# Padding the last 64 tokens to a whole chunk on TensorE, and a plan that lets tiled matmuls follow each other

## The chip, the cores and the metric

The kernel runs on one core of a Trainium2 chip. The metric is the device time of one execution in microseconds. Four engines compute: TensorE (PE in the profile, with its weight loads shown apart as PEld), VectorE (DVE), ScalarE (ACT) and GpSimd (POOL). SyncE (SP) only issues DMA transfers here. Each engine works through its own queue in order and waits on semaphores for the others.

## The reference

The input is 16 images of 56 x 56 pixels with 128 channels in float32. Two layers follow each other.

- Layer 0: a group norm over each image, then attention in shifted windows of 7 x 7 (4 heads of 32 channels, with a position bias and a mask), an output projection, and the residual.
- Layer 1: the 3136 pixels of an image become tokens. A layer norm and a causal linear attention are added (features elu + 1, with running sums over the tokens), then a second layer norm, a 128 x 128 matmul, a batch norm over all tokens of all images, and a recurrence y(t) = sigmoid(w(t) + V y(t-1)) along the tokens; its result is added too.

```python
x = x + _L0_conv_ref(_gn(x), ...)            # windows: q k^T, softmax, times v, w_out
t = _to_tokens(x)
t = t + _L1_attn_ref(_ln_t(t), W, b)         # num/den with cumulative sums of k v^T and k
t = t + _L1_ffn_ref(_ln_t(t), W, V, gamma, beta)   # batch norm, then the recurrence
```

## The kernel before

Everything up to the recurrence is recorded first as steps of a planner (class Plan) and only then emitted. A step names its engine, a cost (how long it holds the engine) and a lag (when its result is ready), a rank, the steps it comes after, and the buffers that it takes and drops. The planner plays the steps through with these costs: every engine takes the ready step of lowest rank whose buffers are free. It does so forwards and backwards up to 30 times, keeps the order that ends first by its own figures, and emits all steps in the order of their starts. So a changed cost gives all five engines a new order of instructions. At run time these orders are fixed; if a step's input is late, its engine stands.

Each image gives the planner three kinds of work:

- turned (line 562 and around it): the image is loaded by groups of tokens into xt_buf, PE transposes each group, ACT copies it into xw_buf, DVE takes statistics; from these come the weights ws and the biases of the window attention (L657 to L706).
- window_row, eight times: DVE gathers a row of 8 windows (gather_windows, L747). PE projects q and k (L757) and v (L784) and makes the scores (L808): 32 matmuls of 32 rows by 49 columns, each on its own tile of the array. DVE adds the mask and finds the maxima, POOL subtracts them, ACT takes exponentials, DVE sums, POOL scales. PE transposes (L863), ACT copies, and PE mixes the values (mix, L882): 32 matmuls of 49 rows by 32 columns. ACT copies the result into oT_buf (L917).
- token_group, seven times: PE projects the windows' output (project, L1054), DVE adds it to the tokens (L1063), then a layer norm (statistics on DVE L958, small steps and the scaling on POOL, L965 to L978, a transpose on PE, L562), feature maps (L1095, ACT L1105 and L1114, DVE L1118), values (L1142), transposed features (L1165), products within a chunk (L1180), the attention from the state and within the chunk (L1209, L1212), the running state (L1220), and after a second layer norm the matmul L1309, whose results are stored for the recurrence.

An image has 3136 tokens: six groups of 4 chunks of 128 tokens, and a last group of one chunk of 64. In that last group the transposes read 64 rows, and the matmuls whose stationary operand is the chunk's tokens have 64 columns. PSUM has 3 single banks (tag b) and 2 double ones (tag a, for scores, transposes, mixes and the token attention), and the planner gives them out.

A float32 matmul appears as two PE instructions, a transpose as one. PE holds 15,735 matmuls and transposes in the program, 27,070 in the profile.

When the plan has ended, the recurrence runs (lines 1464 to 1690): PE, ACT, DVE and the DMA queues in a chain of 112 steps with 16 to warm up.

Of the kernel before, what the change touches and what calls it, by code (L numbers as in the profile page):

```python
# [39 lines left out]
class Step:  # L40


    def __init__(self, engine, cost, rank, emit, after, takes, drops, lag):
        self.engine, self.cost, self.rank, self.emit = engine, cost, rank, emit
        self.takes, self.drops, self.lag = takes, drops, lag
        self.then = []
        self.missing = 0
        for a in after:
            if a is not None:
                a.then.append(self)  # L50
                self.missing += 1


class Plan:
# [8 lines left out]
    AHEAD = 30.0  # L63

# [16 lines left out]
    def run(self, missing, then, rank, gate, begin=None, done=None):  # L81


        events, ready, busy = [], {}, {}
# [14 lines left out]
        while events:  # L99
# [14 lines left out]
            for e, steps in ready.items():  # L114
                if busy[e]:
                    continue
                held, best = [], None
                while steps and best is None:
# [12 lines left out]
                push(t + best.cost, "idle", best)  # L131
                push(t + best.lag + self.HOP, "done", best)
# [74 lines left out]
def tile_conv_attn_hybrid(  # L207
# [32 lines left out]
    assert 0 < T % GT <= CK  # L240
# [36 lines left out]
    def chunks_of(g, xt):  # L277

        return xt[: GROUPS[g][1][0], G * g : G * g + len(GROUPS[g][1]), :]

# [90 lines left out]
    with ExitStack() as s1:  # L371
# [66 lines left out]

        nc.gpsimd.memset(xw_bufs[1], 0.0)
# [118 lines left out]
        def transpose_group(pt, xg):  # L558

            n = xg.shape[0]  # L560
            for cc in range(xg.shape[1]):
                nc.tensor.transpose(  # L562
                    pt[:, n * cc : n * (cc + 1)], xg[:, cc, :], ident[:n, :n]
                )
# [11 lines left out]
        def turned(b, t, loaded, xw_buf, rank):  # L576
# [7 lines left out]
            for g in range(NG):  # L584
# [3 lines left out]
                def turn(g=g, bt=bt):  # L588
                    t0, t1 = group_tokens(g)
                    o[g] = bank(bt, P, t1 - t0)  # L590
                    transpose_group(o[g], chunks_of(g, t["xt"]))
# [17 lines left out]
                def stat(g=g):  # L609
                    if o["st"] is None:  # L610
# [9 lines left out]
                    part(g, (0.43, 0.60), (0.06, 0.23)),  # L620
# [7 lines left out]
                    part(g, (0.62, 0.75), (0.18, 0.30)),  # L628
# [8 lines left out]
                        part(g, (0.62, 0.70), (0.11, 0.19)),  # L637
# [95 lines left out]
        def window_row(b, u, i, o, t, taken, normed, xw_buf, oT_buf, rank):  # L733
# [188 lines left out]
            xk = st("DVE", (0.45, 0.53), rank, gather_windows, [*taken, last_value[i % 2]], drops=[xw_buf])  # L922
# [7 lines left out]
            sc = st("PE", (0.98, 1.06), rank, scores, [q, k, last_turn[i % 2]], takes=[asc], drops=[kT])  # L930
# [10 lines left out]
            mi = st("PE", (0.85, 0.92), rank, mix, [tu, vo], takes=[apa], drops=[pT, v])  # L941
            cost = (0.82, 0.94) if u < NU - 1 else (1.20, 1.32)
# [5 lines left out]
        def layer_scale(t, g, d, key, rank, after, drops=()):  # L948
# [27 lines left out]
            def scale():  # L976
                d["xn"] = own(xn, P, G, C)[:np, :nk]
                nc.gpsimd.tensor_tensor(  # L978
                    d["xn"],
# [5 lines left out]
            def turn():  # L985
                d["pt"] = bank(bt, P, nk * np)
                transpose_group(d["pt"], d["xn"])
# [3 lines left out]
            s = plan.step("POOL", part(g, (2.13, 2.17), (1.20, 1.24)), rank, join, [s])  # L991
            sc = plan.step(
                "POOL",
                part(g, (1.01, 1.05), (0.30, 0.34)),
# [8 lines left out]
                part(g, (0.43, 0.60), (0.06, 0.23)),  # L1003
# [27 lines left out]
        def token_group(b, g, i, t, turned_x, rows_done, oT_buf, xt_buf, rank):  # L1031
# [19 lines left out]
            def project():  # L1051
                d["po"] = bank(bo, np, nk, C)
                for cc in range(nk):
                    nc.tensor.matmul(  # L1054
                        d["po"][:, cc, :],
                        t["oT"][:, t0 + np * cc : t0 + np * (cc + 1)],
# [5 lines left out]
            def plus_attention():  # L1062
# [3 lines left out]
            s0 = st("POOL", part(g, (1.23, 1.27), (0.34, 0.38)), rank - SLOT, plus_bias, [turned_x])  # L1066
            s1 = st(
                "PE",
                part(g, (0.88, 1.04), (0.22, 0.38)),
# [10 lines left out]
            def x_out():  # L1080
                d["xnT"] = own(xnT, P, GT)[:, :nt]
                nc.scalar.copy(d["xnT"], d["pt"])  # L1082
# [6 lines left out]
            def feature(j):  # L1089
# [3 lines left out]
                def proj():  # L1093
# [4 lines left out]
                        d["xnT"],  # L1098
# [17 lines left out]
                def larger():  # L1116
                    d[key] = own(f, P, GT)[:, :nt]
                    nc.vector.scalar_tensor_tensor(  # L1118
                        d[key],
# [7 lines left out]
                p = st("PE", part(g, (0.87, 1.03), (0.12, 0.28)), rank, proj, [xo, *first], takes=[bp], drops=[xnT])  # L1127
                s = st("ACT", part(g, (0.58, 0.68), (0.25, 0.35)), rank, relu, [p], takes=[r])
                s = st("ACT", part(g, (0.53, 0.63), (0.20, 0.30)), rank, expo, [s])
                return st("DVE", part(g, (0.66, 0.75), (0.16, 0.25)), rank, larger, [s], takes=[f], drops=[r, bp]), f  # L1130
# [5 lines left out]
            def chunk(f, cc):  # L1136
                return f[:, np * cc : np * (cc + 1)]

            def values():
                d["pv"] = bank(bv, np, nk, C)  # L1140
                for cc in range(nk):
                    nc.tensor.matmul(  # L1142
                        d["pv"][:, cc, :],
# [15 lines left out]
            s = st("PE", part(g, (0.88, 1.04), (0.22, 0.38)), rank, values, [xo, *first, *last_pd[i % 2]], takes=[bv], drops=[xnT])  # L1159
            vo = st("DVE", part(g, (0.60, 0.69), (0.20, 0.28)), rank, v_out, [s], drops=[bv])  # L1160

            def turn_k():
                d["pk"] = bank(bk, np, nk, C)
# [3 lines left out]
            def k_out():  # L1167
                d["k"] = own(k, P, G, C)[:np, :nk]
# [8 lines left out]
            def products():  # L1177
                d["pA"] = bank(bA, np, nk, np)
                for cc in range(nk):
# [3 lines left out]
                        chunk(d["f0"], cc),  # L1183
# [4 lines left out]
            def A_out():  # L1188
                d["A"] = own(A, P, G, CK)[:np, :nk, :np]
                nc.vector.tensor_tensor(  # L1190
                    d["A"],
                    d["pA"],
                    causal_sb[:np, :np].unsqueeze(1).to_broadcast([np, nk, np]),
# [3 lines left out]
            s = st("PE", part(g, (0.89, 1.05), (0.11, 0.28)), rank, products, [fq, fk], takes=[bA], drops=[bfk])  # L1197
# [5 lines left out]
            def attend(cc):  # L1203
                c = G * g + cc
                if cc == 0:
                    d["pn"] = pairs[apn.place][:np]
                to = d["pn"][:, cc // 2, (C + 1) * (cc % 2) : (C + 1) * (cc % 2 + 1)]
                if c > 0:
# [4 lines left out]
                    to, d["A"][:, cc, :], v1[:np, cc, :], start=c == 0, stop=True  # L1213
                )

            def gather(cc):
                c = G * g + cc
                if c == 0:
# [4 lines left out]
                    v1[:np, cc, :],  # L1223
# [50 lines left out]
            def divisors():  # L1274
                na, ni = max(nk // 2, 1), min(nk, 2)
                pn4 = d["pn"][:, 0:na, 0 : ni * (C + 1)].rearrange(
# [494 lines left out]
```

## Time and profile before

| | |
|---|---|
| median of 3 runs | 1933.95 us (1931.54 to 1940.33) |
| the profiled execution | 1933.64 us, its span 1931.8 us |
| granted clock of TensorE, mean | 0.983 |
| busy, share of the span | PE 96%, PEld 77%, DVE 73%, ACT 68%, POOL 60% |
| planned part | from about 24 us to the first L1521 at 1728.87 us |
| recurrence | from there to the end |

In the profile a line names an instruction's place in the code, its engine, the operation and out<-in by the program's names. The 40 digits of a row are busy tenths in 40 equal slices of the span. The ends of matmuls are modelled, so PE's busy share does not say how much of it is needed; the starts are recorded. In the timeline the columns are start, duration from the first to the last of the merged instructions, engine, line, operation, tile names, rows*columns of the array in use, shape, and count. In the table of groups they are count, then busy us and mean ns of one, then the engine's idle time just before, with what ended it.

### The profile page before, as it was taken

What the parts mean: (1) busy time and instruction counts of PE and PEld (TensorE: products, weight loads), DVE (VectorE), ACT (ScalarE), POOL (GpSimd) and SP (SyncE); (2) the same over time, 40 slices, a digit from 0 to 9 for tenths busy, and PEclk for the clock granted to TensorE, in tenths of its full rate; (3) what the DMA queues carried; (4) which work ended last, traced back from release to release, by engine and by line L of the source; (5) the groups of instructions that cost most, each with busy time, mean ns of one, the idle gap of its engine ahead of it and who ended that gap; (6) DMA issues with size and microseconds to landing.
All of it is one profiled execution on the core that took longest, in us unless ns stands there. A gap on an engine that the chain in (4) does not pass through costs nothing.

```text
span 1931.8 us, 65226 instructions
## 1 busy us (share of the span) xinstructions
PE 1846.2 (96%) x27070; PEld 1489.0 (77%) x27070; DVE 1401.3 (73%) x3227; ACT 1306.1 (68%) x3235; POOL 1159.8 (60%) x2025
## 2 busy tenths in 40 slices
PE   6999999999999999999999999999999999989787
PEld 4878777886887778877878787787878777857666
DVE  5777677777677777776777777767777767757678
ACT  4776766767666777667767676766777766647455
POOL 5766767566667667576767576676757756640000
PEclk8999999999999999999999999999999999989889
DMA  4112121111111121211111111212111020555998
GB/s 134 30 30 70 35 62 36 31 63 41 58 45 48 34 70 30 63 46 59 35 36 58 40 61 33 64 34 65 40 35 42 19 85 19 179 202 191 410 408 291
DMA packets 150462, 160.98 MB, mean 83 GB/s; under 512 B 5456, under 2 KB 134224, under 8 KB 148368
## 3 DMA queue, kind: packets, MB, share of 16 engines
q1 hardware_dynamic: 148576, 155.96, 23.8%
q8 instruction: 215, 3.52, 0.8%
q10 hardware_dynamic: 1584, 0.79, 0.1%
q14 instruction: 87, 0.71, 0.1%
HBM read 80.34 MB, written 76.38 MB: 81 GB/s over the span
## 4 chain that ended last, share of the span: by engine, by line
PE 77%; DVE 8%; ACT 5%; DMA 4%; issue 2%; POOL 2%; SPq 0%; ACTq 0%; DVEq 0%; POOLq 0%
PE bank L757 8%; PE bank L1095 8%; PE bank L784 6%; PE bank L562 6%; PE pair L808 5%; PE pair L863 5%; PE state_bank L1220 5%; PE bank L1054 5%; PE bank L1180 5%; PE pair L1209 4%; PE bank L1142 4%; PE pair L1212 4%; PE pair L882 4%; PE bank L1309 4%; DMA out_dram<-o_a 4%
## 5 line engine op out<-in xcount | busy, mean ns | idle before, releaser
L853 POOL TENSOR_TENSOR p_buf<-p_buf,rc 128x784 f32<-128x784 f32 x128 | 195.1, 1525 | 125.4 <-DVE rc L850 69.5
L834 POOL TENSOR_TENSOR s<-s,mx 128x784 f32<-128x784 f32 x128 | 193.6, 1512 | 102.9 <-DVE mx L831 98.3
L1095 PE MATMUL bank<-xnT,awc_sb 128*128 128x512 f32 (+1 forms) x448 | 210.9, 554 | 2.6 <-ACT xnT L1082 0.9
L1105 ACT ACTIVATE r<-bank,bqk_neg 128x512 f32<-128x512 f32 (+1 forms) x224 | 143.6, 641 | 89.3 <-PE bank L1095 69.8
L1118 DVE SCALAR_TENSOR_TENSOR f<-bank,bqk_one,r 128x512 f32<-128x512 f32 (+1 forms) x224 | 149.9, 669 | 44.3 <-ACT r L1114 36.8
L917 ACT ACTIVATE oT_buf<-pair,gbias 128x28 f32<-128x28 f32 (+4 forms) x576 | 144.1, 354 | 30.6 <-PE pair L882 30.1
L819 DVE TENSOR_TENSOR s<-pair,wmask_sb 128x784 f32<-128x784 f32 x128 | 123.3, 963 | 53.1 <-PE pair L808 41.5
L1209 PEld LDWEIGHTS pair<-state,f 128*128 128x128 f32 (+1 forms) x768 | 121.9, 188 | 48.9 <-issue 29.3
L1220 PE MATMUL state_bank<-v_buf,k 128*128 128x129 f32 x768 | 156.4, 285 | 2.1 <-ACT state L1232 1.7
L1220 PEld LDWEIGHTS state_bank<-v_buf,k 128*128 128x128 f32 x768 | 122.4, 190 | 44.2 <-issue 22.2
L1212 PE MATMUL pair<-v_buf,A 128*128 128x129 f32 (+1 forms) x800 | 155.9, 276 | 0.1
L1209 PE MATMUL pair<-state,f 128*128 128x129 f32 (+1 forms) x768 | 153.5, 281 | 0.3 <-ACT state L1232 0.2
L873 ACT COPY pT<-pair 128x904 f32<-128x904 f32 x128 | 118.5, 926 | 47.5 <-PE pair L863 42.5
L1232 ACT COPY state<-state_bank 128x129 f32<-128x129 f32 x384 | 107.4, 280 | 58.8 <-PE state_bank L1220 54.6
L1044 POOL TENSOR_TENSOR xt_buf<-xt_buf,bout_sb 128x512 f32<-128x512 f32 (+1 forms) x112 | 128.3, 1159 | 30.0 <-PE bank L562 25.9
L1568 ACT ACTIVATE y_a<-z_buf,bsh 128x224 f32<-128x224 f32 x224 | 100.1, 447 | 67.8 <-PE z_buf L1565 66.9
L848 DVE TENSOR_REDUCE sm<-p_buf 128x16 f32<-128x784 f32 x128 | 122.9, 960 | 26.6 <-ACT p_buf L844 25.8
L562 PE MATMUL bank<-ident,xn 128*128 128x128 f32 (+1 forms) x800 | 125.3, 275 | 11.4 <-POOL xn L978 4.0
L1114 ACT ACTIVATE r<-r 128x512 f32<-128x512 f32 (+1 forms) x224 | 130.8, 584 | 3.0
L808 PEld LDWEIGHTS pair<-kT,q_buf 32*49 32x49 f32 x8192 | 105.9, 121 | 30.6 <-issue 18.5
L1565 PE MATMUL z_buf<-y_a,fvT_sb 128*128 128x224 f32 x444 | 127.3, 370 | 0.2 <-ACT y_a L1568 0.2
L831 DVE TENSOR_REDUCE mx<-s 128x16 f32<-128x784 f32 x128 | 122.6, 958 | 1.5
(155 smaller groups left out, 5064.3 us busy)
## 6 DMA issues: line engine op xcount, KB each, us to landing
x_d<-xt_buf SPq DMA_DIRECT2D x96, 256.0 KB, 2.2
xt_buf<-in_x_dram SPq DMA_DIRECT2D x93, 256.0 KB, 2.8
xs_d<-staged SPq DMA_DIRECT2D x15, 1568.0 KB, 6.4
out_dram<-o_a SPq DMA_DIRECT2D x13, 1792.0 KB, 15.3
xw_buf<-x_d SPq DMA_DIRECT2D x8, 2048.0 KB, 22.6
spare<-xs_d SPq DMA_DIRECT2D x4, 1680.0 KB, 17.4
oT_buf<-x_d SPq DMA_DIRECT2D x3, 2048.0 KB, 24.2
xs_ring<-xs_d SPq DMA_DIRECT2D x3, 1680.0 KB, 13.0
```

The lines of the kernel that those rows point to most:

```text
L562: nc.tensor.transpose(pt[:, n * cc : n * (cc + 1)], xg[:, cc, :], ident[:n, :n])
L757: nc.tensor.matmul(d[key], o["ws"][:, j * P : (j + 1) * P], xk, start=True, stop=True)
L808: nc.tensor.matmul(sc[64 * hh : 64 * hh + WT, hp, w * WT : (w + 1) * WT], qT[r : r + HD, w * WT : (w + 1) * WT], d["kT"][r : r + HD, w * W ...
L834: nc.gpsimd.tensor_tensor(d["sf"], d["sf"], d["mx"].unsqueeze(2).to_broadcast([P, nb, WT]), ALU.subtract,)
L853: nc.gpsimd.tensor_tensor(prf, prf, d["rc"].unsqueeze(2).to_broadcast([P, nb, WT]), ALU.mult)
L917: nc.scalar.activation(to, piece, AF.Identity, bias=o["bias"][:, 2:3])
L1095: nc.tensor.matmul(d[f"p{j}"], awc_sb[:, j * P : (j + 1) * P], d["xnT"], start=True, stop=True,)
L1105: nc.scalar.activation(d[f"r{j}"], d[f"p{j}"], AF.Relu, bias=bqk_neg[:, j : j + 1], scale=-1.0,)
L1118: nc.vector.scalar_tensor_tensor(d[key], d[f"p{j}"], bqk_one[:, j : j + 1], d[f"r{j}"], ALU.add, ALU.max,)
L1209: nc.tensor.matmul(to, chunk(d["f0"], cc), t["states"][c], start=True, stop=False)
L1212: nc.tensor.matmul(to, d["A"][:, cc, :], v1[:np, cc, :], start=c == 0, stop=True)
L1220: nc.tensor.matmul(t["pd"], d["k"][:, cc, :], v1[:np, cc, :], start=c == 0, stop=True, skip_group_check=True,)
```

## The change

The last group's single chunk of 64 tokens is handled by PE as a whole chunk. Its transposes read all 128 rows (with zeros or older values behind the tokens), and matmuls whose stationary operand is the chunk take 128 columns; the second half of what comes out is not used. DVE, ACT and POOL still read and write only the 64 tokens. Four memsets at the start make the rows behind the tokens finite. In the planner, scores and mixes are marked as using tiles: after a tiled step PE takes another ready tiled step, if its rank is within 3 of the lowest, and a tiled step behind an untiled one is charged 0.1. Costs and lags of many steps are changed as well.

```diff
+    SWITCH = 0.1
+    NEAR = 3.0
@@ Plan.run
+                if tiles.get(e):
+                    near = sorted(r for r in steps if self.steps[r[1]].tiles)
+                    for r in near:
+                        if r[0] > min(steps)[0] + self.NEAR:
+                            break
+                        s = self.steps[r[1]]
+                        if begin is None or begin(s):
+                            best = s
+                            steps.remove(r)
+                            heapq.heapify(steps)
+                            break
...
-                push(t + best.cost, "idle", best)
-                push(t + best.lag + self.HOP, "done", best)
+                more = self.SWITCH if best.tiles and not tiles.get(e) else 0.0
+                tiles[e] = best.tiles
+                push(t + more + best.cost, "idle", best)
+                push(t + more + best.lag + self.HOP, "done", best)
@@ buffers at the start
+        nc.gpsimd.memset(flat(oT_buf0)[:, T : T + CK], 0.0)
+        for xt in xt_bufs:
+            nc.gpsimd.memset(xt[64:, G * (NG - 1), :], 0.0)
@@ transpose_group
-                    pt[:, n * cc : n * (cc + 1)], xg[:, cc, :], ident[:n, :n]
+                    pt[:, CK * cc : CK * (cc + 1)], xg[:, cc, :], ident
@@ turned
-                    transpose_group(o[g], chunks_of(g, t["xt"]))
+                    xg = whole_chunks(g, t["xt"])
+                    pt = bank(bt, P, CK * xg.shape[1])
+                    o[g] = pt[:, 0 : t1 - t0]
+                    transpose_group(pt, xg)
@@ window_row
-            xk = st("DVE", (0.45, 0.53), rank, gather_windows, ...
+            xk = st("DVE", (0.27, 0.37), rank, gather_windows, ...
-            sc = st("PE", (0.98, 1.06), rank, scores, ...
+            sc = st("PE", (0.88, 0.95), rank, scores, ...
-            mi = st("PE", (0.85, 0.92), rank, mix, ...
-            cost = (0.82, 0.94) if u < NU - 1 else (1.20, 1.32)
+            mi = st("PE", (0.74, 0.81), rank, mix, ...
+            sc.tiles = mi.tiles = True
+            cost = (0.91, 1.04) if u < NU - 1 else (1.47, 1.65)
@@ token_group, project
-                d["po"] = bank(bo, np, nk, C)
+                po = bank(bo, P, nk, C)
+                d["po"] = po[:np]
...
-                        t["oT"][:, t0 + np * cc : t0 + np * (cc + 1)],
+                        t["oT"][:, t0 + CK * cc : t0 + CK * (cc + 1)],
@@ token_group, chunk and products
-                return f[:, np * cc : np * (cc + 1)]
+                return f[:, CK * cc : CK * (cc + 1)]
...
-                        chunk(d["f0"], cc),
+                        chunk(d["f0"], cc)[:, :np],
@@ token_group, attend
-                    d["pn"] = pairs[apn.place][:np]
+                    d["pn"] = pairs[apn.place]
...
-                    to, d["A"][:, cc, :], v1[:np, cc, :], start=c == 0, stop=True
+                    to, d["A"][:, cc, :], v1[:, cc, :], start=c == 0, stop=True
```

The values (L1142) and the tiles k, A and xnT are widened in the same way. Costs of the last group are raised: its transposes from 0.06 to 0.11, its small POOL steps (L965 to L972) from 1.20 to 1.61, and others alike.

## The prediction

> **What bounds the kernel now.** I read the page first, then busy time by stage, then PE's waits, then PE's timeline at the places where the tile shape changes.
>
> ```profile
> span 1931.8 us, 65226 instructions
> ...
> PE 1846.2 (96%) x27070; PEld 1489.0 (77%) x27070; DVE 1401.3 (73%) x3227; ACT 1306.1 (68%) x3235; POOL 1159.8 (60%) x2025
> ...
> PE   6999999999999999999999999999999999989787
> ...
> PEclk8999999999999999999999999999999999989889
> ```
>
> ```profile
> 500.00:900.00 400.00, 394.50 (x6107) 319.36 (x6110) 295.42 (x713) 281.66 (x707) 274.50 (x479) 1.00 0.15 46
> ...
> 1860.00:1932.00 72.00, 58.10 (x364) 50.17 (x364) 57.34 (x96) 39.80 (x89) 0.00 (x0) 0.91 0.87 328
> ```
>
> The second fence gives per stretch the busy time of PE, PEld, DVE, ACT and POOL, the granted clock, the share of the DMA engines and GB/s. From about 24 us to 1729 us the planned part runs: PE is busy in 394.5 of 400 us at clock 1.00, while DVE (295), ACT (282) and POOL (275) have a quarter or more of their time free. From 1729 us on the recurrence runs, some 203 us, with the DMA engines at 0.87 to 1.02; no instruction of it is changed. So the planned part ends when PE has got through its list, and the question is what PE's list costs.
>
> A busy PE hides how. One matmul's record is longer than the time it holds its successor up, so I measure each group of matmuls by its **slot**: from its first start to the first start of the next group. PE's timeline shows them:
>
> ```profile
> 883.92 0.39 PE L1212 MATMUL pair<-v_buf,A 128*128 128x129 f32 x2
> 884.24 0.27 PE L562 MATMUL bank<-ident,xn 64*128 64x64 f32 x1
> 884.44 0.49 PE L1220 MATMUL state_bank<-v_buf,k 128*128 128x129 f32 x2
> 884.86 0.81 PE L882 MATMUL pair<-pT,v 49*32 49x49 f32 x64
> 885.60 0.93 PE L757 MATMUL bank<-oT_buf,ws 128*128 128x392 f32 x2
> 886.36 1.05 PE L1180 MATMUL bank<-f,f 128*128 128x128 f32 x8
> 887.25 1.06 PE L1054 MATMUL bank<-wout_sb,oT_buf 128*128 128x128 f32 x8
> 888.14 0.39 PE L1220 MATMUL state_bank<-v_buf,k 128*128 128x129 f32 x2
> 888.46 0.43 PE L1142 MATMUL bank<-awc_sb,xnT 128*64 128x128 f32 x2
> 888.82 0.49 PE L1209 MATMUL pair<-state,f 128*128 128x129 f32 x2
> 889.15 0.39 PE L1212 MATMUL pair<-v_buf,A 128*128 128x129 f32 x2
> 889.37 0.33 PE L1095 MATMUL bank<-xnT,awc_sb 128*128 128x64 f32 x2
> ```
>
> Read the starts (the numbers behind MATMUL are rows*columns of the array in use). L1212 among full groups (889.15 to 889.37) takes 0.22 us. L1212 ahead of a tiled group (883.92 to 884.24) takes 0.32, L1209 behind one (888.82 to 889.15) 0.33, L1220 between two of them (884.44 to 884.86) 0.42. Over all groups of the planned part the medians are sharp: **entering** a tile shape adds 0.093 us to the full group before it, and **leaving** adds 0.103 us to the full group after it (0.055 where that is a transpose, L562, L863, L1165). The tiled groups hold PE for 0.878 (scores, L808) and 0.738 (mix, L882) whatever stands beside them, the 14 places where these two already touch included. The pieces of the last 64 tokens take 0.202 (L562), 0.363 (L1054, L1142), 0.364 (L1209), 0.361 (L1212) and 0.258 (L1180); a full chunk takes 0.109 for a transpose and 0.223 for a matmul.
>
> **PE's whole list before**, by these slots over the built program's order: full groups 1331.9, scores 112.4 (128 x 0.878), mixes 94.5, last-64 pieces 37.1, 323 entries 30.0 (x 0.093), 323 exits 30.3 (262 x 0.103 + 61 x 0.055); together 1636.2 us. The planned part lasts about 1705 us, so PE stands or is held some 70 us in it: about 4%, spread thin, as PE's longest waits show only a few us each.
>
> **The change, part by part.** *Last 64 tokens padded to a whole chunk.* The matmul count stays 15,735. Per image there are 3 transposes and 5 matmuls of the mini group. Before: 48 x 0.202 + 32 x 0.363 + 16 x (0.364 + 0.361 + 0.258) = 37.1. After: 48 x 0.109 + 64 x 0.223 + 16 x 0.167 = 22.2; L1180 now streams only 64 columns in full shape, for which I take the 64-column L1095 (0.165 to 0.169). Saved: 14.9 us.
>
> *Entries and exits.* In the built order of the new program no mini group leaves the full shape, and 43 scores and mixes stand directly behind each other, against 14. Excursions fall from 323 to 213. Entries 19.8, exits 165 x 0.103 + 48 x 0.055 = 19.6; together 39.4 against 60.4. Saved: 20.9 us. Leaving the old order and only dropping the mini groups' own excursions (81 consist of nothing else) gives about 15.4 of it; pairing the tiled groups gives the other 5.5.
>
> So PE's list becomes 1636.2 - 35.8 = 1600.4 us.
>
> *A rule against the padding.* The Trainium skill, "TensorE: Matmul & The Clock Gate", section on LDWEIGHTS, says that the load of the stationary operand takes time by its columns, whatever its rows. Five matmuls of two passes in 16 images then load 128 columns in place of 64, and the trace agrees on the length:
>
> ```profile
> L1142 PEld LDWEIGHTS bank<-awc_sb,xnT 128*128 128x128 f32 x768 | 95.3, 191 | 21.9 <-issue 8.5 <-ACT staged L1329 4.5 <-DVE f L1118 2.2
> ...
> L1142 PEld LDWEIGHTS bank<-awc_sb,xnT 128*64 128x64 f32 x32 | 3.1, 134 | 2.2 <-issue 0.6
> ```
>
> By the rule alone that is 160 x 57 ns = 9 us lost, and the saving 26.7. By the row, a pass of full shape starts 0.111 us after the last although its load is 0.191 long: the load lies under the matmul before. The tiled pass takes 0.181 with a load of 0.134: it does not. I take the row, and keep 9 us for the range.
>
> *Re-plan.* All orders are new. SP keeps its issues, with the same sequence at the end; ACT, DVE and POOL keep their counts and shapes. What may move is the 70 us of stalls. For: the planner's new figures stand nearer to the rows (a mix's output copies now 0.91 and 1.47, slots 0.91 and 1.48; before 0.82 and 1.20). Against: pulling a mix forward to follow its scores lets PE meet an unfinished copy: 4 of the 14 touching pairs waited, 0.57 us together, so 29 more at 0.04 cost 1.2 us. And from a window's scores to its transposes PE now has 12.3 us of its own list on average, before 13.0; the work between (two DVE passes, POOL, ACT, DVE, POOL) needs some 7.5. I put 3 us on that, between -10 and +18.
>
> *A rule against the re-plan.* The gathers of windows (L747) are planned at 0.27 us, before at 0.45.
>
> ```profile
> L747 DVE COPY x_buf<-xw_buf 128x392 f32<-128x392 f32 x64 | 46.8, 732 | 23.9 <-PE bank L784 17.6 <-POOL xw_buf L653 6.0
> L747 DVE COPY oT_buf<-xw_buf 128x392 f32<-128x392 f32 x64 | 40.1, 627 | 13.6 <-PE bank L784 13.5
> ```
>
> The median is 0.37 and the longest 4.83. "SBUF — State Buffer", the section on its two sides, says that DVE and GpSimd hold a shared port pair exclusively, and the loser waits for the other's whole instruction; the long gathers here do run beside a POOL operation of 1.5 us. Against its plan a gather runs 0.41 late on average, before 0.23; 128 x 0.18 = 23 us more of unplanned DVE time, with mask additions and maxima queued behind it and PE's transposes behind those. If all of it reached PE the saving would be 13 us; DVE's free quarter says little of it does, since the same 0.23 x 128 = 29 us lie in a total of 70 now. It is inside the +18 end.
>
> *The start.* Four new memsets on POOL and PE's wait for them: POOL's small memsets take 0.10 to 0.20, so 0.8 us at most, ahead of 4.1 us in which POOL idles for a load; the x3_d padding store waits for the next memset, which ended at 6.2 while SP came to that store at 13.0. Cost nothing; without that cover 0.8 us. On DVE the mask addition (0.96) now stands ahead of the step that leads to the first weights, in place of one gather: +0.6. On PE the centring matmuls move from behind L692 into PE's 8.0 us wait for the weights: -1.7. Together -1.
>
> **Sum** against the profiled execution, 1933.6 us: -35.8 - 1.0 + 1.2 + 3 = 1901.0. The median of the runs is 0.3 above it; I round to **1902 us**, 1.7% less.
>
> **The rivals.**
> (a) *Stalls eat half.* PE's list is 35.8 shorter, but chains through DVE and POOL set the pace where they are tight; for it, POOL's busy share and the gathers; against it, a free quarter on each. Stalls 70 to 88: about 1917.
> (b) *More than the sum.* The planner's truer figures cut the stalls by 10 to 12: about 1889. Nothing in the trace shows which stalls came from wrong figures.
> (c) *No effect.* PE's slots shrink but each PE step waits for another engine at the same hour: 1934. Against: PE waits for others only a few us in the planned part.
> (d) *Slower.* Gathers land beside POOL operations more often, their mean goes from 0.68 to 1.5 us (128 x 0.82 = 105 us of DVE time), and half of it reaches PE through the queue on DVE: 1934 - 36 + 52 = 1950. It decides once over a third, 0.28 us per gather, gets through.
>
> **How the numbers follow.** Likeliest case 61% (own range 1894 to 1911), (a) 16%, (b) 12%, (c) 4%, (d) 7%. Some 0.5% (9.7 us) is what a measurement of this kernel can tell from no change. Faster 0.89, same 0.04, slower 0.07. The range 1888 to 1921 takes in most of (a) and (b), and the 9 us of weight loads.
>
> **What would show it.** In the profile after: no rows of 64 for L562, L1054, L1142, L1180, L1209, L1212; their slots 0.109, 0.223 and 0.167; PE instructions unchanged at 27070; the planned part ending near 1697, the recurrence still 203 us long. If weight loads of the padded chunks were not hidden, slots of 0.28 instead of 0.223 would say so. The forecast is wrong if PE's waits for copies and transposes grow by more than some 15 us in the planned part, or if the mean of the gathers passes 1 us and DVE's releases head PE's waits.

## The result, and the profile after

The changed kernel takes **1907.78 us** (median of 4 runs, 1907.02 to 1910.34) against 1935.89 us (1931.54 to 1940.33) for the kernel before, run beside it: 0.986 of it, 95% interval 0.984 to 0.988. The forecast was 1902, range 1888 to 1921: right in sign, inside the range, 5.8 us too low. The profiled execution of the changed kernel took 1908.29 us.

The page of the changed kernel, first the span and the busy time of the engines, then PE's row and its clock over 40 slices:

```profile
span 1906.4 us, 65252 instructions
...
PE 1819.7 (95%) x27070; PEld 1490.2 (78%) x27070; DVE 1396.6 (73%) x3227; ACT 1302.8 (68%) x3235; POOL 1161.0 (61%) x2029
...
PE   6999999999999999999999999999999999988888
...
PEclk8999999999999999999999999999999999989889
```

PE's instructions are the 27070 of before, its busy time is 26.5 us less, and the clock is granted as before. POOL has four instructions more (the memsets); the other engines have the same counts and within 5 us the same busy time.

The busy time by stretch of the changed kernel (PE, PEld, DVE, ACT, POOL, then the granted clock, the DMA share and GB/s):

```profile
500.00:900.00 400.00, 390.90 (x6161) 320.05 (x6160) 296.79 (x704) 283.40 (x713) 271.81 (x468) 1.00 0.16 50
```

In the same 400 us PE is busy 3.6 us less than before: it stands more often.

PE's timeline of the changed kernel at two places, with the slots that were forecast (start of the group, length, engine, line, operation, rows*columns of the array in use):

```profile
1162.32 0.82 PE L785 MATMUL bank<-x_buf,ws 128*128 128x392 f32 x2
1162.98 0.38 PE L1085 MATMUL bank<-wout_sb,oT_buf 128*128 128x128 f32 x2
1163.20 0.39 PE L1252 MATMUL state_bank<-v_buf,k 128*128 128x129 f32 x2
1163.88 1.12 PE L1126 MATMUL bank<-xnT,awc_sb 128*128 128x512 f32 x2 [0.29 <-ACT kT L800]
```

```profile
886.73 0.27 PE L588 MATMUL bank<-ident,xn 128*128 128x128 f32 x1
886.84 0.88 PE L785 MATMUL bank<-oT_buf,ws 128*128 128x392 f32 x2
887.65 0.95 PE L836 MATMUL pair<-kT,q_buf 32*49 32x49 f32 x64
888.53 0.81 PE L910 MATMUL pair<-pT,v 49*32 49x49 f32 x64
889.26 0.70 PE L1126 MATMUL bank<-xnT,awc_sb 128*128 128x512 f32 x1
```

The padded piece of L1085 (L1054 before) holds PE for 0.22 us, from 1162.98 to 1163.20, where it held it for 0.363. The single padded transpose (L588, before L562) holds it for 0.11, from 886.73 to 886.84, where it held it for 0.202. At 887.65 a mix (L910) stands directly behind a scores group (L836), and the two keep 0.88 and 0.73 us. In the first fence there is also something new: two groups behind the padded piece, PE stands idle for 0.29 us ahead of L1126. That is where a part of the gain went.

With the method of the forecast (slots by kind over the trace, from 24 us to the first matmul of the recurrence) the time divides like this:

| us, profiled execution | before | after | difference | forecast |
|---|---|---|---|---|
| PE's list, as found in the trace | 1633.4 | 1597.6 | -35.8 | -35.8 |
| PE held or standing beyond it (stalls) | 73.2 | 84.5 | +11.3 | +4.2 |
| first 24 us | | | -1.0 | -1.0 |
| recurrence starts at | 1728.9 | 1703.4 | -25.5 | 1697 |
| recurrence and what follows it | 202.9 | 203.1 | +0.2 | 0 |
| whole execution (1.8 us beyond the span) | 1933.6 | 1908.3 | -25.3 | 1901.0 |

The list shrank as worked out. All of the 7 us that are missing lie in one term: the stalls grew by 11.3 us, not by 4.2. The waits of PE in the changed kernel (line waited at, releaser, total, times, longest) show no single new wait:

```profile
PE bank L720 <- ACT ws L715: 6.1, 1, 6.1
PE bank L588 <- POOL xn L1007: 4.7, 2, 4.3
PE bank L588 <- DMA xt_buf<-in_x_dram: 4.7, 1, 4.7
...
PE bank L785 <- DVE bst L1344: 3.0, 5, 0.9
...
PE bank L1341 <- ACT xfT L1337: 2.3, 6, 0.7
...
PE bank L588 <- DVE gst L642: 1.4, 4, 0.5
...
PE bank L812 <- DVE gst L642: 1.2, 4, 0.4
```

The same places in the kernel before:

```profile
PE bank L692 <- ACT ws L687: 8.0, 1, 8.0
...
PE bank L562 <- DMA xt_buf<-in_x_dram: 4.5, 1, 4.5
PE bank L562 <- POOL xn L978: 4.0, 2, 3.8
...
PE bank L562 <- DVE gst L614: 1.7, 5, 0.8
...
PE bank L757 <- DVE bst L1312: 0.8, 2, 0.6
```

The first, at the start, fell from 8.0 to 6.1 us, since the centring matmuls now run in that time. The next two stood in the kernel before as well. After them come waits of a few tenths each, and among these the ones for a PSUM bank that the statistics of VectorE (bst, gst) had still to read have grown: from 24 us to the recurrence they sum to 4.6 us before and 9.3 after. So two theories stood:

- **A, the re-plan**, as the forecast put it: the stalls come from the new order, and the padding alone would bring its whole list.
- **B, the shorter list**: PE gets sooner to places where the data or the bank comes at a time that other engines set, so the padding hands a part back in any order.

And under either: which of the other engines' work is it that PE waits for?

### The profile page after: what moved, and what is told of

It reads as the page before. It is cut to its first block, busy times and chain, and to the rows that moved or that the text cites. A ratio compares the mean times of both kernels' runs of the same rounds, so it can differ in the third digit from the quotient of the medians.

```text
span 1906.4 us, 65252 instructions
## 1 busy us (share of the span) xinstructions
PE 1819.7 (95%) x27070; PEld 1490.2 (78%) x27070; DVE 1396.6 (73%) x3227; ACT 1302.8 (68%) x3235; POOL 1161.0 (61%) x2029
## 4 chain that ended last, share of the span: by engine, by line
PE 79%; DVE 8%; ACT 6%; DMA 3%; issue 2%; POOL 1%; SPq 0%; ACTq 0%; DVEq 0%; POOLq 0%
PE bank L1126 8%; PE bank L785 8%; PE bank L588 6%; PE bank L812 5%; PE pair L836 5%; PE pair L891 4%; PE bank L1212 4%; PE pair L1241 4%; PE state_bank L1252 4%; PE bank L1174 4%; PE bank L1085 4%; PE pair L1244 4%; PE bank L1341 4%; PE pair L910 4%; PE z_buf L1597 3%; DMA out_dram<-o_a 3%
## 5 line engine op out<-in xcount | busy, mean ns | idle before, releaser
L1126 PE MATMUL bank<-xnT,awc_sb 128*128 128x512 f32 (+1 forms) x448 | 211.3, 554 | 2.4 <-DVE f L1149 1.3
L1241 PEld LDWEIGHTS pair<-state,f 128*128 128x128 f32 x768 | 123.8, 191 | 43.1 <-issue 28.7
L1244 PE MATMUL pair<-v_buf,A 128*128 128x129 f32 x800 | 155.0, 275 | 0.5 <-DVE A L1222 0.5
L1241 PE MATMUL pair<-state,f 128*128 128x129 f32 x768 | 152.8, 281 | 0.2
L588 PE MATMUL bank<-ident,xn 128*128 128x128 f32 x800 | 126.5, 277 | 8.9 <-POOL xn L1007 4.7
L836 PEld LDWEIGHTS pair<-kT,q_buf 32*49 32x49 f32 x8192 | 105.6, 120 | 31.7 <-issue 17.4
L1244 PEld LDWEIGHTS pair<-v_buf,A 128*128 128x128 f32 x800 | 121.8, 192 | 4.2 <-issue 1.9
```

What stands on the lines that cost most here:

```text
L588: nc.tensor.transpose(pt[:, CK * cc : CK * (cc + 1)], xg[:, cc, :], ident)
L836: nc.tensor.matmul(sc[64 * hh : 64 * hh + WT, hp, w * WT : (w + 1) * WT], qT[r : r + HD, w * WT : (w + 1) * WT], d["kT"][r : r + HD, w * W ...
L1126: nc.tensor.matmul(d[f"p{j}"], awc_sb[:, j * P : (j + 1) * P], d["xnT"][:, :nt], start=True, stop=True,)
L1241: nc.tensor.matmul(to, chunk(d["f0"], cc), t["states"][c], start=True, stop=False)
L1244: nc.tensor.matmul(to, d["A"][:, cc, :], v1[:, cc, :], start=c == 0, stop=True)
```

## Experiments: the two parts apart

First the padding without the new order. All figures of the planner are those of before, and nothing marks scores and mixes as tiles, so every engine's order is that of the kernel before; the padding of the diff stays.

```diff
-            sc.tiles = mi.tiles = True
-                    part(g, (0.44, 0.60), (0.11, 0.28)),
+                    part(g, (0.43, 0.60), (0.06, 0.23)),
...
```

> Only the padding: shapes of the last 64 tokens and the four memsets as in the change, every planner figure as before, so that all five engines keep the order of before instruction by instruction. My theory (the time is PE's list by slots, plus stalls that belong to an order): the list falls from 1636.2 to 1605.7 (14.9 by slots, 15.6 by 81 excursions less), stalls of 73 rise by 2 to 5 because the same helpers have less time: 1906 to 1911. Rival, the gain is the truer planner figures: about 1935. Rival, the gain is the pairing of scores and mixes: about 1930 or above.

Then the reverse, the new order without the padding: the narrow last 64 tokens of before, with the changed kernel's figures and marks.

```diff
-                    pt[:, CK * cc : CK * (cc + 1)], xg[:, cc, :], ident
+                    pt[:, n * cc : n * (cc + 1)], xg[:, cc, :], ident[:n, :n]
...
```

> Only the new plan: all planner figures and the pairing rule of the change, but the last 64 tokens in narrow shape as before; every engine has the order of the changed kernel. My theory: the list is 1629.6, 6.6 less than before, but the stalls of this order are 84 to 85 and not 73: 1936 to 1941, no gain. Rival, the new plan carries the gain: 1908 to 1915.

The changed kernel without the marks (the planner neither seeks pairs nor charges the switch), and the kernel before with the new costs and lags alone:

```diff
-            sc.tiles = mi.tiles = True
```

> The changed kernel without the marks on scores and mixes: no pairing rule and no charge of 0.1 for entering, all else as changed. 18 touching pairs in place of 43; the list is 1604.8, 4.4 more than with pairs. My theory: 1908 plus 4.4 plus whatever stalls this third order has, 1905 to 1917. Rival, pairing carries the gain: 1925 or more.

```diff
-            xk = st("DVE", (0.45, 0.53), rank, gather_windows, ...
+            xk = st("DVE", (0.27, 0.37), rank, gather_windows, ...
...
```

> The kernel before with the new planner figures alone: narrow shapes, no pairing. The list is 1634.8, 1.4 less than before. My theory: 1935 plus or minus 12, by the stalls of this order. Rival, the truer figures cut the stalls: under 1925.

Measured (list worked out from the built program by the forecast's slots; stalls and the start of the recurrence from the one profiled execution; time as the median of all runs; ratio to the kernel before with its 95% interval):

| kernel | list | stalls | recurrence starts at | time | ratio |
|---|---|---|---|---|---|
| before | 1636.2 | 73.2 | 1728.9 | 1934.6 | |
| padding, old order | 1605.7 | 87.1 | 1712.6 | 1915.3 | 0.990 (0.988 to 0.992) |
| narrow, new order | 1629.6 | 75.3 | 1723.0 | 1928.5 | 0.998 (0.997 to 0.999) |
| padding, new figures, no marks | 1604.8 | 91.4 | 1714.6 | 1921.5 | 0.993 (0.991 to 0.995) |
| narrow, new figures, no marks | 1634.8 | 78.3 | 1731.2 | 1939.0 | 1.002 (1.001 to 1.004) |
| changed kernel | 1600.4 | 84.5 | 1703.4 | 1907.8 | 0.986 (0.984 to 0.988) |

The first two times miss what I expected of them from theory A, 1906 to 1911 and 1936 to 1941; the third lies 4.5 us above its range, and only the fourth is inside. The start of the recurrence is the more direct measure of the planned part: in the profiled executions of all fourteen kernels the recurrence took between 201.4 and 213.8 us, though no kernel changes it, so a few us of a time can come from there.

Read the pairs that share one order. In the old order the padding shortens the list by 30.5 us; the recurrence starts 16.3 sooner, the time falls by 19.3 (15 to 24 by its interval), and the stalls grow by 13.9. In the new order it shortens the list by 29.2; the recurrence starts 19.6 sooner, the time falls by 20.7 (18 to 28 by the two ratios with their intervals), and the stalls grow by 9.2. The new order by itself shortens the list by 6.6 and the time by 6.1, with 2 us more of stalls. So theory A falls: **in either order the padding hands back 9 to 14 us, a third to nearly a half of what it takes off PE's list**, and the re-plan as a whole costs 2 us of stalls. Theory B is the one left; a further run below bears on it.

By parts, the new figures alone add 4.4 us (narrow, 1 to 8 by the interval) and 6.2 us (padded, not clear of the noise); the recurrence starts 2.4 and 2.0 us later. The marks take off 10.5 and 13.8 us, 8.3 and 11.2 of it by the start of the recurrence, which is more than the 5.2 and 4.4 us by which they shorten the list. Whether that is a virtue of the marks, or luck of the orders they led to, these runs can't say; the margin below shows how far an order alone moves the time.

## Where it is handed back

The narrow kernel in the new order and the changed kernel have the same order on PE, so their traces can be laid beside each other group by group. PE's timeline of the narrow one, at the place of the first timeline above:

```profile
1174.63 0.82 PE L773 MATMUL bank<-x_buf,ws 128*128 128x392 f32 x2
1175.39 0.43 PE L1071 MATMUL bank<-wout_sb,oT_buf 128*64 128x128 f32 x2
1175.75 0.49 PE L1237 MATMUL state_bank<-v_buf,k 128*128 128x129 f32 x2
1176.19 1.13 PE L1112 MATMUL bank<-xnT,awc_sb 128*128 128x512 f32 x2
1177.15 1.05 PE L800 MATMUL bank<-ws,oT_buf 128*128 128x128 f32 x8
```

And the next line of the changed kernel there:

```profile
1163.88 1.12 PE L1126 MATMUL bank<-xnT,awc_sb 128*128 128x512 f32 x2 [0.29 <-ACT kT L800]
1164.84 1.05 PE L812 MATMUL bank<-ws,oT_buf 128*128 128x128 f32 x8
```

Narrow, the stretch from L773 to L800 takes 1177.15 - 1174.63 = 2.52 us. Padded, the same stretch (L785 to L812) takes 1164.84 - 1162.32 = 2.52 us. The padded piece and its two neighbours need 0.34 us less by their slots, yet L1126 starts no sooner behind L785: it waits until ScalarE's copy of the keys (L800) releases its bank. These are ScalarE's copies at that place, narrow and then padded:

```profile
1174.84 0.90 ACT L1346 COPY staged<-bank 128x96 f32<-128x96 f32 x3 [0.28 <-PE bank L1326]
1175.53 0.61 ACT L788 ACTIVATE kT<-bank,gbias 128x392 f32<-128x392 f32 x1
```

```profile
1162.52 0.90 ACT L1361 COPY staged<-bank 128x96 f32<-128x96 f32 x3 [0.28 <-PE bank L1341]
1163.22 0.60 ACT L800 ACTIVATE kT<-bank,gbias 128x392 f32<-128x392 f32 x1
```

Counted from the start of PE's projection (L773, L785), these copies begin 0.21 and 0.90 us later in the one kernel and 0.20 and 0.90 in the other, and PE's L1112 or L1126 starts 1.56 us later in both. So here the time is set by a chain that PE's own matmuls start ahead of the piece, and that comes back to PE through ScalarE after the same 1.56 us. The narrow piece and its change of shape had nearly filled that time; the padded piece leaves a hole in it.

Laid beside each other over the whole planned part, the stalls of matched groups grow by 9.2 us. 8.2 of it lie in the slots of the padded pieces and of the two groups behind each, which are 343 of the 3,068 groups. In the old order 5.9 us of its 13.9 lie there; the rest is spread.

Does it come back if PE's list is made longer again? The next kernel is the padded one in the old order, with the last 64 tokens' matmuls of L1067, L1156 and L1194 made four times each, which puts 29.4 us back on the list.

```diff
-                for cc in range(nk):
+                for cc in [0] * 4 if nk == 1 else range(nk):
```

> The padded kernel in the old order (the first experiment), with three of the padded matmuls (output projection, values, products of the last 64 tokens) each made four times into the same place: 144 more matmuls of 0.223 or 0.167, nothing else longer. PE's list goes from 1605.7 to 1635.1, that is back to that of before (1636.2), still in full shape. Theory now, a shorter list uncovers the helpers' time, in any order and whatever shortened it: stalls return from 87 to about 74, 1932 to 1938. Rival, the padded chunks themselves make PE wait (wider reads, more dependencies): stalls stay at 87, 1944 to 1948.

It took 1939.7 us (ratio 1.003, 1.002 to 1.004) on a list of 1635.1, with stalls of 80.9: between the two expectations. Against the padded kernel without the repeats, the 29.4 us more on the list start the recurrence 23.3 us later and lengthen the time by 24.4, and 6.2 of the 13.9 us of stalls go away. The other 7.7 stay, and the kernel is 4.6 us slower than the one before, on a list of almost the same length. So the length of the list alone accounts for less than half of what was handed back in this order. Either it matters where the list is short (the repeats lengthen three of the eight pieces, and not the changes of shape), or the padded pieces bring waits of their own; no run here parts these two.

## What PE waits for

PE's waits named the statistics. Two kernels in the order of the changed kernel take VectorE's time off, at different places. The first takes the group-norm and the batch statistics over 64 of 512 columns, and so leaves out most of both:

```diff
-                        o["st"][:, g, :], o[g]
+                        o["st"][:, g, :], o[g][:, 0:64]
...
-                nc.vector.bn_stats(bst[:, b * NG + g, :], d["pw"])
+                nc.vector.bn_stats(bst[:, b * NG + g, :], d["pw"][:, 0:64])
```

> The changed kernel with the two statistics that DVE takes straight from a single PSUM bank (L642 and L1344) taken over 64 of the 512 columns; this leaves out most of the group norm's and batch norm's statistics. Same orders, same list of PE; DVE is 192 x 0.47 = 90 us shorter, all of it where it holds a bank. Theory, PE's stalls are mostly waits for one of the three single banks (39 of 84 us by the releases in the trace, 22 of them DVE's): stalls fall by 10 or more, under 1899. Rival, the stalls are chains of data through the softmax: 1903 or more.

The second computes the sums and reciprocals of the softmax for one of the two halves of the heads and uses them for both, and so leaves out half of the sums:

```diff
-                nc.vector.tensor_reduce(d["sm"], prf, AX.X, ALU.add)
+                nc.vector.tensor_reduce(d["sm"][:, 0:NW], prf[:, 0:NW], AX.X, ALU.add)
...
```

> The changed kernel with the softmax sums and reciprocals of only the first half of the heads, used for both halves (POOL scales in two halves of the same total); this leaves out half of the sums. DVE is 128 x 0.5 = 64 us shorter, none of it holding a single bank, on the chain from scores to transposes. Theory of the banks: stalls fall by less than 5, 1903 to 1909. Rival, chains through the softmax: down by 8 or more, under 1900.

The short statistics took 1886.3 us (1884.2 to 1890.7; ratio 0.975, 0.973 to 0.977): 21.5 below the changed kernel, stalls 60.8. The short sums took 1904.5 (0.984, 0.982 to 0.986): 3.3 below, stalls 80.0, though some 58 us of VectorE's busy time are gone from the planned part. This cut is not a clean one. POOL, which comes next on the same chain, now scales in two instructions (changed kernel, then short sums):

```profile
L881 POOL TENSOR_TENSOR p_buf<-p_buf,rc 128x784 f32<-128x784 f32 x128 | 195.2, 1525 | 128.1 <-DVE rc L878 77.0 <-ACT r L1136 8.2 <-DVE A L1222 7.0
```

```profile
L883 POOL TENSOR_TENSOR p_buf<-p_buf,rc 128x392 f32<-128x392 f32 x256 | 214.0, 857 | 101.6 <-DVE rc L878 71.7 <-DVE A L1227 3.7 <-PE state_bank L1257 3.7
```

That puts 18.8 us back, so the chain is some 40 us shorter and not 58. The groups of the statistics, first of the changed kernel, then with the short ones (count, busy us and mean ns, then VectorE's idle time ahead of them):

```profile
L1344 DVE BATCH_NORM_STATS2 bst<-bank 128x6 f32<-128x512 f32 (+1 forms) x112 | 70.1, 626 | 62.5 <-PE bank L1341 43.4 <-ACT staged L1361 17.5 <-PE state_bank L1252 0.6
L642 DVE BATCH_NORM_STATS2 gst<-bank 128x6 f32<-128x512 f32 (+1 forms) x112 | 68.4, 624 | 34.4 <-ACT xw_buf L634 24.9 <-PE bank L588 7.9 <-ACT xw_buf L632 0.5
```

```profile
L1344 DVE BATCH_NORM_STATS2 bst<-bank 128x6 f32<-128x64 f32 x112 | 25.4, 227 | 64.1 <-PE bank L1341 44.0 <-ACT staged L1361 18.4 <-PE state_bank L1252 0.6
L642 DVE BATCH_NORM_STATS2 gst<-bank 128x6 f32<-128x64 f32 x112 | 25.3, 227 | 49.5 <-ACT xw_buf L634 35.0 <-PE bank L588 10.2 <-ACT state L1264 1.8
```

138.5 us became 50.7: of 88 us of VectorE's time about a quarter reached the end, against 3 of some 40 us of the chain in the other place. So the place matters, and the statistics are where VectorE holds one of the three single PSUM banks. But the short statistics change both, the hold and the time. To part them, the statistics are next taken over a constant block in SBUF, in the same order; that leaves out both statistics of the data, keeps VectorE's instruction and takes its hold off the bank:

```diff
-                        o["st"][:, g, :], o[g]
+                        o["st"][:, g, :], (ident.unsqueeze(1).to_broadcast([P, 4, P]) if o[g].shape[1] > P else ident[:, 0:64])
...
-                nc.vector.bn_stats(bst[:, b * NG + g, :], d["pw"])
+                nc.vector.bn_stats(bst[:, b * NG + g, :], (ident.unsqueeze(1).to_broadcast([P, 4, P]) if nt > P else ident[:, 0:64]))
```

> The changed kernel in its own order on every engine, where the group-norm and the batch statistics are taken over a constant block of SBUF (the identity, four times over) instead of over the bank: leaves out both statistics of the data. VectorE's instructions stay as long (about 0.69 us each, 105 of 512 elements and as many more in the other place), but VectorE no longer holds the single PSUM bank; only ScalarE's copy does. Theory (it is the hold on the three single banks that stalls TensorE): most of the 21.5 us that the short statistics took off come off here too, so 1886 to 1896 us, stalls near 62 to 72 us. Rival (it is VectorE's time, whatever it reads, that comes late): 1904 to 1911 us, stalls near 84.

```profile
L1344 DVE BATCH_NORM_STATS2 bst<-ident 128x6 f32<-128x512 f32 (+1 forms) x112 | 67.9, 607 | 0.0
L642 DVE BATCH_NORM_STATS2 gst<-ident 128x6 f32<-128x512 f32 (+1 forms) x112 | 65.8, 607 | 0.0
```

VectorE works 607 ns on each, against 625 (means over the full groups of 512 columns and the last ones of 64), and the time is 1887.6 us (1884.4 to 1896.6; ratio 0.976, 0.974 to 0.977), stalls 62.0. Nearly the whole gain of the short statistics is there with VectorE's time left in place. It is the hold on the bank, or the wait of VectorE for PE that goes with it (the idle time ahead of both groups is now 0.0), and not the time that VectorE works. The two are not parted here. PE's waits of this kernel no longer name bst or gst; the largest that the bank of L785 keeps is this:

```profile
PE bank L785 <- ACT staged L1361: 0.9, 3, 0.5
```

Now the question that this left: is what the padding hands back handed back at those banks? The same constant block, in the narrow kernel in the new order:

```diff
-                        o["st"][:, g, :], o[g]
+                        o["st"][:, g, :], (ident.unsqueeze(1).to_broadcast([P, 4, P]) if o[g].shape[1] > P else ident[:, 0:64])
...
```

> The narrow last 64 tokens in the new order, with both statistics taken over the constant block in SBUF (leaves out both statistics of the data). It stands to the padded kernel with the constant block (1887.6 us) as the narrow last 64 tokens in the new order stand to the changed kernel: the same order, TensorE's list longer by 29.2 us (1629.6 against 1600.4). With the statistics on the banks those 29.2 us were worth 20.7 us of time. Theory (the part given back is given back at the banks that VectorE's statistics hold): without that hold the padding is worth nearly its whole list, so 1887.6 + 26 to 30 = 1914 to 1918 us. Rival (a shorter TensorE waits more for anything, so the same third is given back): 1887.6 + 19 to 22 = 1907 to 1910 us.

It took 1905.4 us (1904.0 to 1906.1; ratio 0.985, 0.983 to 0.987), stalls 50.5. So the padding is worth 1905.4 - 1887.6 = 17.8 us here (12 to 23 by the two ratios with their intervals; the recurrence starts 17.3 us sooner), out of 29.2 on the list, and the stalls grow by 11.5 us. My theory for this run fell, and the time lies even a little under the rival's: taking the statistics off the banks lowers the stalls (75 to 50 narrow, 84 to 62 padded), but it does not lower what a shorter list hands back. Of the 11.5 us, 7.0 lie again in the padded pieces' slots and the two groups behind them; 2.5 are one wait at L1212, 3.8 us against 1.3, for which the profile names no releaser.

A planner's figure, for scale: the changed kernel with 0.30 us in place of 0.12 added to every lag behind an engine other than PE.

```diff
-    MARGIN = 0.12
+    MARGIN = 0.30
```

> The changed kernel with the planner's allowance for late results (MARGIN) at 0.30 in place of 0.12; nothing is left out. List 1601.8. If stalls are helpers that run later than planned, a larger allowance gives an order with more distance and stalls of 65 to 78: 1890 to 1903. If the orders' stalls are scatter, 1903 to 1922.

It took 1917.9 us (0.991, 0.989 to 0.994), stalls 93.4 on a list of 1601.8. One figure of the planner moves the time by 10 us, all in stalls: what the order alone does is as large as most of the terms that I summed.

## A version that beats both

The hold can go without leaving anything out. ScalarE copies both banks to SBUF anyway, so the statistics can be taken from the copies: the group-norm statistics from eight rows of 56 tokens of xw_buf at a time, the batch statistics from four columns of 112 tokens of the staged outputs. Both steps then follow the copy and no longer drop the bank; the planner makes a new order. First the group-norm statistics alone:

```diff
-                        o["st"][:, g, :], o[g]
+                        o["st"][:, g, :],
+                        image_rows(xw_buf)[:, KB * g : KB * (g + 1), 0:W],
...
-                        [pe],
-                        drops=[bt],
+                        [cp],
+                        drops=[xw_buf],
```

> The changed kernel with the group-norm statistics taken from the copied rows in SBUF (eight rows of 56 at a time, after ScalarE's copy) instead of from the bank of the transposes; nothing is left out, and the planner makes a new order from that. TensorE's list 1599.9 against 1600.4 us. Theory (hold on the banks): about half of the statistics' share, 7 to 13 us, comes off: 1895 to 1901 us. Rival (the statistics come later by ScalarE's copy, VectorE takes as long, and the port that VectorE shares with GpSimd makes them longer): 1907 to 1918 us.

It took 1908.1 us (0.987, 0.986 to 0.989), stalls 84.1: no gain. That is the rival's time, but not its reason: VectorE's instructions did not get longer (617 ns over 448 columns of SBUF, 692 before over 512 of the bank). The order is new as well, so a gain of some us may be hidden in its scatter. With the batch statistics as well, for all images but the last:

```diff
-                nc.vector.bn_stats(bst[:, b * NG + g, :], d["pw"])
+                if b == B - 1:
+                    nc.vector.bn_stats(bst[:, b * NG + g, :], d["pw"])
+                else:
+                    nc.vector.bn_stats(
+                        bst[:, b * NG + g, :], staged[:, :, 4 * g : 4 * g + 4]
+                    )
...
+            if b < B - 1:
+                bs = st("DVE", (0.61, 0.70), rank, batch_stats, [xs], drops=[t["xs_buf"]])
```

> As the last, and the batch statistics too are taken from the staged outputs in SBUF (four columns of 112 at a time, after ScalarE's copy) for all images but the last; nothing is left out. List 1600.1 us. Theory (hold on the banks): 1885 to 1897 us. Rival (VectorE's time and the port): 1907 us or more, and the new order's own scatter of some 8 us either way is the least difference that says anything.

It took **1891.8 us** (1890.8 to 1897.5; ratio 0.979, 0.977 to 0.981), 16.0 below the changed kernel, with the whole computation done. List 1600.1, stalls 66.2: the gain is stalls alone. The groups, now off the banks for all but the last image:

```profile
L642 DVE BATCH_NORM_STATS2 gst<-xw_buf 128x6 f32<-128x448 f32 x112 | 67.2, 616 | 30.7 <-ACT xw_buf L632 29.9 <-ACT xw_buf L634 0.3
L1348 DVE BATCH_NORM_STATS2 bst<-staged 128x6 f32<-128x448 f32 x105 | 64.5, 614 | 22.4 <-ACT staged L1367 21.7
L1346 DVE BATCH_NORM_STATS2 bst<-bank 128x6 f32<-128x512 f32 (+1 forms) x7 | 4.4, 629 | 8.9 <-PE bank L1342 8.9
```

The batch statistics from the staged outputs alone were not run, so whether the second half carries the whole gain, or only an order in which it could, stays open. 16 us is more than the 10 that the margin moved, but not so much more that the new order can be left out as a part of it.

## Why the prediction was right, and where it was off

- **PE bounds the planned part, so its list counts.** Right: in all four pairs of kernels with the same order the shorter list gave the shorter time, and in the two profiled executions the recurrence took 202.9 and 203.1 us.
- **The slots, 14.9 us for the pieces and 20.9 for entries and exits.** Right: where nothing waits the padded pieces take 0.109, 0.223 and 0.170; entering and leaving cost 0.093 and 0.103 (0.055) as before; the trace has the 213 excursions and the 43 touching pairs; and with these the list falls by 35.8 us.
- **Weight loads of padded chunks.** I took the row over the rule of "TensorE: Matmul & The Clock Gate", and the row held. PEld's group of the padded L1174 now counts 800 loads of one length,

```profile
L1174 PEld LDWEIGHTS bank<-awc_sb,xnT 128*128 128x128 f32 x800 | 99.9, 192 | 16.6 <-issue 7.2 <-ACT kT L800 2.0 <-ACT q_buf L790 1.1
```

  the 32 of 134 ns became 192 ns long as the rule says, and the slot was 0.223: the 9 us did not come. My 0.181 for a narrow pass was a mean: the second pass starts 0.160 us after the first, and the next group 0.203 after that, a change of shape included. So it did not show by itself that a narrow load lies bare.
- **Re-plan, +3 us, and +1.2 for pairs.** This is the step that failed, in size and in its reason. The stalls grew by 11.3 us and not by 4.2. The re-plan with its pairs brought 2 of that; the padding in one and the same order brought 9 to 14. I had charged the stalls to the new order only and costed the padding at its whole list, as if no chain through another engine had been hidden behind the narrow pieces. That a shorter list gives a part back is what rival (a) said, at 18 us; but its chains through DVE and POOL are not shown to be the ones, and the one place laid open here goes through ScalarE. That the re-plan's 2 us stand near my 4.2 is in part luck: they are the sum of about +5 from the new figures and -3 from the marks.
- **Truer figures of the planner.** I left them open between -10 and +18; alone they put 2 us on the planned part and 4 to 6 on the time. Rival (b), that they cut the stalls, got nothing: by themselves they raised them by 4 to 5.
- **The gathers, rival (d).** Their groups after:

```profile
L775 DVE COPY x_buf<-xw_buf 128x392 f32<-128x392 f32 x64 | 41.5, 648 | 30.5 <-PE bank L812 23.5 <-POOL xw_buf L681 6.0 <-POOL ld_a L994 0.7
L775 DVE COPY oT_buf<-xw_buf 128x392 f32<-128x392 f32 x64 | 40.3, 630 | 16.4 <-PE bank L812 16.3
```

  Their mean went from 0.68 to 0.64 us and the longest from 4.83 to 2.16. Planning them shorter did not make them meet POOL more often: 30 of the 128 took over 1 us in each kernel. Every one of these ends 0.22 us behind the end of a POOL operation, before and after, which agrees with what "SBUF — State Buffer" says of the shared port, but the new order brought no more of them.
- **The start.** -1.0 us as forecast. With the padding alone, in the old order, the first matmul that waits for the weights came at 21.54 us against 21.49, so the memsets cost next to nothing; and in the new order the centring matmuls run before it.

The sign was earned by the list, and so was the place inside the range; the missing 7 us are the stalls' term. What is not settled is which chains take it back: the growth lies right behind the padded pieces in the new order, less than half of it does in the old, and no one releaser heads it.

## What to carry to other kernels

Where one engine is busy 96% of the time, a cut of its list need not be worth its whole length: in three pairs of kernels with the same order, 29 to 30 us off the list gave 18 to 21 us, each known to some 5 us, and in a fourth, lengthened elsewhere by 29 us, 24 us arrived. So ask of a slow piece which chain runs behind it, from the engine through a helper and back, and charge the rest of that chain to the cut and not only to a new order. The same VectorE instructions cost this kernel 20 us more where they read a scarce PSUM bank than where they read a constant in SBUF: look at who drops a bank last. Reading from a copy that exists anyway gained nothing in one new order and 16 us in another. And put the scatter of a planner's orders, some 10 us here for one figure, beside every term of the sum that is smaller.

## What was not expected of the hardware

The price of changing the tile shape is a constant of this kernel to a few nanoseconds: 0.093 us on the full group before and 0.103 us (0.055 for a transpose) on the one after, the same in the kernel before and in the changed one, and a mix directly behind scores pays nothing (0.878 and 0.738 us, as anywhere else). VectorE's statistics over 512 columns take 693 ns from a PSUM bank and 673 ns from SBUF, and 615 ns over 448 columns of SBUF, so moving them off the bank cost VectorE nothing.
